# Layer 3's windowed attention in query blocks of ten rows, with another order of work on near tiles

## The chip, the cores and the metric

The kernel runs on one core of a Trainium2 chip. The metric is the device time of one execution in microseconds (us). Before the change it is 3778.4 us, the median of three runs (3774.7 to 3779.35). The engines are TensorE (PE in the profile, its weight loads PEld), VectorE (DVE), ScalarE (ACT), GpSimd (POOL) and SyncE (SP), which issues the DMAs.

## The reference, cut to what matters

Four layers run one after another on `x` of shape (4, 256, 48, 48), each of the form `x = x + layer(group_norm(x))`. Layers 0 to 2 are convolutions, and the change doesn't touch them. Layer 3 is a linear attention with eight heads of 32 channels and three square windows:

```python
q = sigmoid(einsum('bchw,oc->bohw', x, Wq)).reshape(b*h, d, H, W)
k = sigmoid(einsum('bchw,oc->bohw', x, Wk)).reshape(b*h, d, H, W)
v = normalized over the head's channels (einsum('bchw,oc->bohw', x, Wv))
Ik  = integral(k)                                    # 2D running sums
Ikv = integral(einsum('bfhw,bghw->bfghw', k, v))
for w in (1, 2, 4):
    ws  = H // w                                     # windows of 48, 24 and 12
    wk  = box(Ik, ws);  wkv = box(Ikv, ws)           # sums over the window around each pixel
    attn = einsum('bdhw,bdfhw->bfhw', q, wkv)
    norm = einsum('bdhw,bdhw->bhw', q, wk)
    outs.append(attn / (norm[:, None] + 1e-6))
return einsum('bchw,oc->bohw', concatenate(outs), Wout) + bout
```

A sum over a window of `(q.k) v` is the same as masked scores times values. The kernel computes it in that form: scores of all keys against all queries, times a 0/1 mask for each window, times `v`.

## The kernel before

Keys come in tiles of 128: 8 rows x 16 columns (`a` is the block of rows, `c` the column third). Queries come in blocks of 8 rows, `rb`, with 48 columns. The half-widths of the windows are 24, 12 and 6, so a tile is *near* when the narrowest window (`wi` = 2) sees it, and *far* otherwise. For each tile, TensorE computes scores of four heads as two pairs, each pair in a tile of two PSUM banks; VectorE and ScalarE move them into `sm`, one for each window, under the masks; GpSimd makes the narrowest window's from the widest one's; and two tiles later (`LAG`) TensorE multiplies them with `v` into three accumulators.

```python
RB = 8; NRB = H // RB; NB = RB * W
HALVES = [24, 12, 6]; KC = P // RB; LAG = 2

# pools of layer 3
tc.tile_pool(name="kvp", bufs=2 * NRB, ...)          # keys and values of a block of rows
tc.tile_pool(name="smp", bufs=2 * (LAG + 1), ...)    # masked scores
tc.tile_pool(name="ps_s", bufs=2, space=PSUM, ...)   # scores: one tile of two banks for a pair
tc.tile_pool(name="ps_acc", bufs=1, space=PSUM, ...)

# ... cut ...
def rows_seen(wi, a, rb):
    h = HALVES[wi]
    return (max(0, a * RB - h + 1 - rb * RB), min(RB, a * RB + RB + h - rb * RB))

# Block.scores(pr, a, c): for each pair pr a PSUM tile s
for j in range(2):
    head = slice((2 * pr + j) * D, (2 * pr + j + 1) * D)
    pe.matmul(s[:, j, 0 : (r1 - r0) * (c1 - c0)],
              kvs[self.b, self.ct, a][0][head, c, :],
              self.qs[head, r0:r1, c0:c1], start=True, stop=True)

# Block.masked(a, c, ss)
f0, f1 = max(0, c * KC + KC - HALVES[0]), min(W, c * KC + HALVES[0] + 1)
full = abs(a - rb) * RB + RB <= HALVES[0]     # every row of the block sees all rows of the tile
many = seen(NW - 1, a, rb)                    # near

def middle(s, tiles):      # the second window, on VectorE, straight from the bank
    if full and many:
        of_banks(s, tiles, 1, rows_seen(1, a, rb), cols_seen(1, c))
def copy(s, tiles):        # the widest window where no mask is needed, on ScalarE
    if full:
        act.copy(view(tiles, 0, (r0, r1), (f0, f1)), s[:, :, :, f0 - c0 : f1 - c0])
def widest(s, tiles):      # the rest of the widest window, on VectorE
    if not full:
        of_banks(s, tiles, 0, *all0)
        return
    for p0, p1 in ((c0, f0), (f1, c1)):
        if p0 < p1:
            of_banks(s, tiles, 0, (r0, r1), (p0, p1))

first, second = zip(ss, pairs)
copy(*first)
middle(*second)
copy(*second)
middle(*first)
widest(*first)
widest(*second)
for tiles in pairs:
    # GpSimd: the narrowest window (near) or the second one (far), from the widest
    ...

# the main loop: near and far tiles of a block alternate
ss = [blocks[i].scores(pr, a, c) for pr in range(NPR)]
ahead.append(blocks[i].masked(a, c, ss))
if n >= LAG:
    for wi in (1, 0, 2):
        if wi in sms[0]:
            blocks[i].sums(wi, a, c, sms)      # of the tile two places back
advance()                                      # a step of the jobs beside it
```

The jobs that `advance` moves on are the projections of the next image, the running sums of the keys (`k_sums`), the norms (`norms`) and the output of finished blocks (`finish`). They share the engines with the main loop.

Of the kernel before, what the change touches and what calls it, by code (L numbers as in the profile page):

```python
# [21 lines left out]
P = 128  # L22
B, C, H, W = 4, 256, 48, 48
HW = H * W
# [56 lines left out]
NKT = NRB * NKC  # L81

# [63 lines left out]
def conv_preact_kernel(  # L146
# [76 lines left out]
    o_d = [dram.tile([NRB, P, NW * NB], F32, tag=f"o{b}", name=f"o_d{b}") for b in range(B)]  # L223
    n_d = [dram.tile([NRB, HEADS, NW, NB], F32, tag=f"n{b}", name=f"n_d{b}") for b in range(B)]
    r_d = [dram.tile([NRB, HEADS, NW, NB], F32, tag=f"r{b}", name=f"r_d{b}") for b in range(B)]
# [1257 lines left out]
    with (  # L1483
        tc.tile_pool(name="wts3", bufs=1, reuse_waits="tile") as wts,
        tc.tile_pool(name="kvp", bufs=2 * NRB, reuse_waits="tile") as kvp,
# [21 lines left out]
        zeros = wts.tile([P, NB], BF16, name="zeros")  # L1507
# [63 lines left out]
        def norms(b, rb):  # L1571


            sums = []

            def load(ct):
                chans = slice(ct * P, (ct + 1) * P)
                hi = scr.tile([P, NW, RB, W], F32, tag="nhi", name="nhi")
                lo = scr.tile([P, NW, RB, W], F32, tag="nlo", name="nlo")
                qf = scr.tile([P, RB, W], F32, tag="nq", name="nq")  # L1580
                sync.dma_start(
                    out=qf.rearrange("p r w -> p (r w)"),
                    in_=q_d[b][chans, rb * NB : (rb + 1) * NB],
                )
                for wi, h in enumerate(HALVES):

                    y0 = rb * RB + h - 1
                    n = max(0, min(RB, H - y0))
                    if n > 0:
                        sync.dma_start(  # L1590
                            out=hi[:, wi, 0:n], in_=kb_d[b][wi, chans, y0 : y0 + n, :]
                        )
                    if n < RB:
                        sync.dma_start(
                            out=hi[:, wi, n:RB],
                            in_=kb_d[b][wi, chans, H - 1 : H, :].to_broadcast([P, RB - n, W]),
                        )

                    y0 = rb * RB - h - 1
                    n = min(RB, max(0, -y0))  # L1600
                    if n < RB:
                        sync.dma_start(
                            out=lo[:, wi, n:RB], in_=kb_d[b][wi, chans, y0 + n : y0 + RB, :]
                        )
                return hi, lo, qf

            last = min(rb + HALVES[0] // RB, NRB - 1)
            yield from wait_for(
                *((what, b, ct, at) for what, at in (("kb", last), ("q", rb)) for ct in range(NCT))
            )  # L1610
            loaded = [load(ct) for ct in range(NCT)]
            yield FETCH
            for hi, lo, qf in loaded:
                for wi, h in enumerate(HALVES):
                    n = min(RB, max(0, h + 1 - rb * RB))
                    if n < RB:
                        pool.tensor_sub(hi[:, wi, n:RB], hi[:, wi, n:RB], lo[:, wi, n:RB])
                yield 1
                for wi in range(NW):
                    pool.tensor_mul(hi[:, wi], hi[:, wi], qf)  # L1620
                sums.append(hi)
                yield 1
            yield 1
            yield from bank(1)
            ps = ps_m.tile([P, 512], F32, tag="st", name="norm_ps")
            for ct in range(NCT):
                for wi in range(NW):
                    pe.matmul(
                        ps[D * wi : D * (wi + 1), 0:NB],
                        head_sel[:, ct, :],  # L1630
                        sums[ct][:, wi].rearrange("p r w -> p (r w)"),
                        start=(ct == 0),
                        stop=(ct == NCT - 1),
                    )
            yield 1
            ns = scr.tile([D * NW, NB], F32, tag="ns", name="ns", bufs=1)
            act.copy(ns, ps[0 : D * NW, 0:NB])
            yield 1
            for wi in range(NW):
                sync.dma_start(out=n_d[b][rb, :, wi, :], in_=ns[D * wi : D * wi + HEADS])  # L1640
            nn = HEADS * NW * NB // P
            nr = scr.tile([P, nn], F32, tag="nr", name="nr")
            flat = [d[b][rb].rearrange("h w n -> (h w n)") for d in (n_d, r_d)]
            sync.dma_start(out=nr, in_=flat[0].rearrange("(p n) -> p n", n=nn))
            yield FETCH
            dve.tensor_scalar_add(nr, nr, ATTN_EPS)
            dve.reciprocal(nr, nr)
            yield 1
            sync.dma_start(out=flat[1].rearrange("(p n) -> p n", n=nn), in_=nr)
            made.add(("norm", b, rb))  # L1650
# [12 lines left out]
        def load_q(b, ct, rb):  # L1663
            qs = qp.tile([P, RB, W], F32, tag="qs", name="qs")
            sync.dma_start(
                out=qs.rearrange("p r w -> p (r w)"),
                in_=q_d[b][ct * P : (ct + 1) * P, rb * NB : (rb + 1) * NB],
            )
            return qs

        def rows_seen(wi, a, rb):

            h = HALVES[wi]
            return (
                max(0, a * RB - h + 1 - rb * RB),
                min(RB, a * RB + RB + h - rb * RB),
            )
# [5 lines left out]
        class Block:  # L1683


            def __init__(self, b, ct, rb, qs):
                self.b, self.ct, self.rb, self.qs = b, ct, rb, qs
                self.tiles = tiles_of(rb)
                self.todo = [
                    [(a, c) for a, c in self.tiles if seen(wi, a, rb)] for wi in range(NW)  # L1690
                ]
                self.accs = self.stage = None

# [18 lines left out]
            def masked(self, a, c, ss):  # L1712
# [8 lines left out]
                            [P, 2, RB, min(W, KC + 2 * HALVES[wi])],  # L1721
# [15 lines left out]
                def times_mask(engine, wi, rows, cols, dst, src):  # L1737
                    mr = rb * RB + rows[0] - (a * RB - HALVES[wi] + 1)
# [14 lines left out]
                full = abs(a - rb) * RB + RB <= HALVES[0]  # L1753
# [7 lines left out]
                def copy(s, tiles):  # L1761
                    if full:
                        act.copy(
                            view(tiles, 0, (r0, r1), (f0, f1)), s[:, :, :, f0 - c0 : f1 - c0]
                        )

                def widest(s, tiles):
# [3 lines left out]
                    for p0, p1 in ((c0, f0), (f1, c1)):  # L1771
                        if p0 < p1:
                            of_banks(s, tiles, 0, (r0, r1), (p0, p1))
# [4 lines left out]
                copy(*first)  # L1778
                middle(*second)
                copy(*second)  # L1780
                middle(*first)
                widest(*first)
# [13 lines left out]
            def begin(self):  # L1796
                self.accs = [
                    ps_acc.tile([P, NB], F32, tag=f"acc{i}", name=f"acc{i}") for i in range(NW)
                ]
                self.stage = op.tile([P, NW, NB], F32, tag="stage", name="stage")  # L1800

                for acc in self.accs[1:]:
                    pe.matmul(acc, zeros[:, 0:P], zeros, start=True, stop=False)
# [23 lines left out]
        def tiles_of(rb):  # L1827
# [4 lines left out]
                for a in sorted(range(NRB), key=lambda a: abs(a - rb))  # L1832
# [8 lines left out]
        def prepare(i):  # L1841

            b, ct, rb = order[i]
            yield from wait_for(("norm", b, rb))
            yield from take("o")
            o = op.tile([P, NW, NB], F32, tag="o", name="o", bufs=1)
            sync.dma_start(out=o.rearrange("p w n -> p (w n)"), in_=o_d[b][rb])
            yield from take("res")
            res = scr.tile([P, NCT, RB, W], F32, tag="res", name="res")
            sync.dma_start(  # L1850
                out=res,
                in_=x3_d[b][:, rb * RB : (rb + 1) * RB, :].rearrange("(ct p) r w -> p ct r w", p=P),
            )
            rcs = []
            for t in range(NCT):
                yield from take("rc")
                rc = op.tile([P, NW, NB], F32, tag="rc", name="rc")
                for g in range(HG):
                    sync.dma_start(
                        out=rc[g * D : (g + 1) * D].rearrange("p w n -> p (w n)"),  # L1860
                        in_=r_d[b][rb, t * HG + g]
                        .rearrange("w n -> (w n)")
                        .partition_broadcast(D),
# [4 lines left out]
        def finish(i, stage):  # L1868


            b, ct, rb = order[i]
            yield 1
            if ct == 0:
                sync.dma_start(out=o_d[b][rb], in_=stage.rearrange("p w n -> p (w n)"))
# [11 lines left out]
            for mo in range(NCT):  # L1886
                yield from bank(2)
                ps = ps_m.tile([P, 512], F32, tag="st", name="out_ps")[:, 0:NB]
# [18 lines left out]
                out=out[b, :, rb * RB : (rb + 1) * RB, :].rearrange("(ct p) r w -> p ct r w", p=P),  # L1907
# [4 lines left out]
        order = [(b, ct, rb) for b in range(B) for ct in range(NCT) for rb in range(NRB)]  # L1912
# [11 lines left out]
        seen_first = HALVES[0] // RB + 1  # L1924
# [6 lines left out]
        LOADS = {2: (0,), 3: (1, 2), 4: (3, 4), 5: (5,)}  # L1931
# [20 lines left out]
        def midway(i):  # L1952

            b, ct, rb = order[i]
            if (b, ct) == (0, 0) and 0 < rb <= NRB - seen_first:
                a = seen_first - 1 + rb
                until(("k", 0, 0, a), ("v", 0, a))
                load_kv(0, 0, a)
            if ct == NCT - 1:
                start(prepare(i))  # L1960
            if i + 1 < len(order):
                nb, nct, nrb = order[i + 1]
                until(("q", nb, nct, nrb))
# [88 lines left out]
```

## Time and profile before

| what | before |
|---|---|
| time, median of 3 | 3778.4 us |
| span of the profiled execution | 3775.4 us |
| TensorE / VectorE / ScalarE / GpSimd busy in the span | 86% / 66% / 27% / 40% |
| layer 3: first scores to the last instruction | 1429.5 to 3771.8 us |
| score matmuls in the trace | 5760, busy 832.5 us |
| sums into the accumulators in the trace | 13440, busy 880.5 us |
| VectorE's masks out of the banks | 2592, busy 1135.8 us |
| ScalarE's copies out of the banks | 1152, busy 594.9 us |
| GpSimd's masks | 1152, busy 853.3 us |

Busy time is the union of the records of a group, so matmuls that overlap count once. Each f32 matmul of the program shows as two records in the trace. All instructions carry line 142, that of a helper that records them, so groups are told apart by their tiles: `s` is scores, `sm` masked scores, `acc` the accumulators, `stage` a finished block. In the group lines, the number after the bar is busy time and mean duration in ns, then the idle time of the engine just before and what ended it. A line of the timeline has start, duration, engine, operation and count, and in brackets the idle time before it with its releaser.

### The profile page before, as it was taken

The numbers are of one execution on the slowest core, as the hardware profiler recorded it, in microseconds if no ns is written. First come the engines' busy times: TensorE is split into PE (matmuls) and PEld (weight loads), VectorE is DVE, ScalarE is ACT, GpSimd is POOL, SyncE is SP. The second block draws the span as 40 slices with busy tenths as digits, with TensorE's granted clock in tenths as the row PEclk, the third lists the DMA queues.
The fourth block names the chain that finished last, engine by engine and source line by source line (L and its number), as shares of the span: only waits on it lengthen the run. The fifth ranks groups of instructions, "written<-read, shape, count | busy, mean of one in ns | idle before, by whom it ended". The sixth has DMA issues, their size and how long they took to land. (4 is left out here: it accounts for less than half of the span.)

```text
span 3775.4 us, 68847 instructions
## 1 busy us (share of the span) xinstructions
PE 3264.8 (86%) x26498; PEld 1879.4 (50%) x26498; DVE 2487.2 (66%) x5119; ACT 1036.2 (27%) x2025; POOL 1518.1 (40%) x2184
## 2 busy tenths in 40 slices
PE   3688898998996788988889889899899899989998
PEld 2467686786784564433334334344443344444443
DVE  7876587587583366777666567756577766556665
ACT  0012111111113322433222333332344332233331
POOL 0000120020020034778765486755365766344332
PEclk9798999999997899999999899999999999999999
DMA  7745323324324313345434243533223444101122
GB/s 250 238 135 170 100 104 116 109 95 125 109 75 124 102 70 108 125 136 159 125 103 131 90 136 122 164 97 108 78 95 123 139 116 116 47 31 53 41 60 60
DMA packets 373019, 423.04 MB, mean 112 GB/s; under 512 B 129076, under 2 KB 328532, under 8 KB 371540
## 3 DMA queue, kind: packets, MB, share of 16 engines
q1 hardware_dynamic: 371491, 416.32, 35.6%
q8 instruction: 211, 3.46, 0.4%
q0 software_dynamic: 144, 1.52, 0.2%
q14 instruction: 117, 0.95, 0.1%
q10 hardware_dynamic: 1056, 0.79, 0.1%
HBM read 288.79 MB, written 131.25 MB: 111 GB/s over the span
## 5 line engine op out<-in xcount | busy, mean ns | idle before, releaser
L142 DVE TENSOR_TENSOR sm<-s,masks 128x112 f32<-128x112 f32 (+10 forms) x2592 | 1135.8, 493 | 765.5 <-PE s L142 321.1
L142 POOL TENSOR_TENSOR sm<-sm,masks 128x432 f32<-128x432 f32 (+14 forms) x1152 | 853.3, 755 | 936.5 <-ACT sm L142 672.0
L142 PE MATMUL s<-qs,ks 32*128 32x320 f32 (+3 forms) x5760 | 832.5, 500 | 200.1 <-DVE sm L142 151.2
L142 ACT COPY sm<-s 128x528 f32<-128x528 f32 (+2 forms) x1152 | 594.9, 535 | 1470.7 <-PE s L142 1169.9
L142 PE MATMUL acc<-sm,vs 128*32 128x384 f32 (+18 forms) x13440 | 880.5, 385 | 16.1 <-POOL sm L142 15.8
L142 PEld LDWEIGHTS s<-qs,ks 32*128 32x128 f32 x5760 | 374.1, 185 | 604.7 <-DVE sm L142 232.8
L142 PE MATMUL cv<-vx,wt 128*128 128x288 f32 x2080 | 559.3, 425 | 90.7 <-DVE vx L142 49.1
L142 PEld LDWEIGHTS acc<-sm,vs 128*32 128x32 f32 x13440 | 355.2, 110 | 551.3 <-issue 348.6
L142 PEld LDWEIGHTS cv<-vx,wt 128*128 128x128 f32 x2080 | 402.4, 198 | 212.4 <-issue 53.6
L142 POOL MEMSET v<- 128x16 f32 (+1 forms) x120 | 18.6, 215 | 725.7 <-DVE vx L142 635.7
L142 PE MATMUL cv<-v,wl 128*128 128x384 f32 x1152 | 224.5, 354 | 24.4 <-DVE x L142 9.2
L142 PEld LDWEIGHTS cv<-v,wl 128*128 128x128 f32 x1152 | 214.8, 195 | 34.6 <-issue 16.1
L142 POOL TENSOR_TENSOR pt<-pt 128x144 f32<-128x144 f32 x336 | 187.4, 558 | 22.8 <-DVE pt L142 0.5
L142 POOL TENSOR_TENSOR v<-l2v,v 128x384 fp32r<-128x384 f32 x96 | 109.2, 1168 | 130.2 <-ACT v L142 121.4
L142 POOL TENSOR_TENSOR nhi<-nhi,nq 128x384 f32<-128x384 f32 x144 | 148.3, 1058 | 0.0
L142 PE MATMUL cv<-pad,wl 128*128 128x384 bf16 x864 | 143.1, 327 | 0.0
L142 PE MATMUL out_ps<-o,wout_sb 128*128 128x384 f32 x288 | 122.8, 509 | 9.4 <-DVE o L142 5.4
L142 PE MATMUL out_ps<-stage,wout_sb 128*128 128x384 f32 x288 | 117.3, 489 | 0.4 <-DVE stage L142 0.4
L142 PE MATMUL proj_ps<-wv_sb,xn 128*128 128x256 f32 x288 | 89.5, 438 | 32.3 <-ACT vt L142 19.1
L142 DVE TENSOR_TENSOR vx<-v 128x868 f32<-128x868 f32 x112 | 115.4, 1056 | 0.5
L142 PE MATMUL ap<-seen,xT 120*128 120x120 f32 (+3 forms) x832 | 113.5, 293 | 0.0
L142 PEld LDWEIGHTS <-wl 128*128 128x128 bf16 x864 | 83.8, 97 | 59.1 <-issue 0.4
(162 smaller groups left out, 2859.0 us busy)
## 6 DMA issues: line engine op xcount, KB each, us to landing
wt<-wt SPq DMA_DIRECT2D x48, 768.0 KB
kb_d<-pt SPq DMA_DIRECT2D x48, 576.0 KB
rc<-r_d SPq DMA_DIRECT2D x192, 144.0 KB
nhi<-kb_d SPq DMA_DIRECT2D x120, 192.0 KB
nlo<-kb_d SPq DMA_DIRECT2D x88, 192.0 KB
o_d<-stage SPq DMA_DIRECT2D x24, 576.0 KB
o<-o_d SPq DMA_DIRECT2D x24, 576.0 KB
wl<-wl_d SPq DMA_DIRECT2D x16, 768.0 KB
```

The source lines that it names most:

```text
L142: return lambda *args, **kwargs: self.tc.keep_in_program_order(op(*args, **kwargs))
```

## The change

There are two parts. First, the query blocks of the main loop become ten rows high (`QR`, so five blocks, the last one of eight rows); keys, projections and norms stay in blocks of eight. ScalarE's copy is decided row by row: the rows `g0` to `g1` that see the whole key tile are copied if they are more than a third, and VectorE masks the other rows. Second, on near tiles VectorE begins with the first pair and ScalarE with the second, and then they change banks. Both are for fewer and larger instructions and for shorter times in which one engine waits for another's bank.

What goes with it: keys and values get nine buffers instead of twelve, and their loads for the next half are issued a block earlier; the norms load the second operand one half at a time into one buffer; the reciprocals go to memory in an order that a block of ten rows can be read from, in eight stores instead of one.

```diff
+QR = 10
+QROWS = [(y, min(H, y + QR)) for y in range(0, H, QR)]
+NQB = len(QROWS)
+QN = QR * W
...
-        tc.tile_pool(name="kvp", bufs=2 * NRB, reuse_waits="tile") as kvp,
+        tc.tile_pool(name="kvp", bufs=NRB + 3, reuse_waits="tile") as kvp,
...
         # norms
+                lo = scr.tile([P, NW, RB, W], F32, tag="nlo", name="nlo", bufs=1)
...
+            lo = load_less(0)
             yield FETCH
-            for hi, lo, qf in loaded:
+            for ct, (hi, qf) in enumerate(loaded):
+                if ct > 0:
+                    yield FETCH
...
+                if ct + 1 < NCT:
+                    lo = load_less(ct + 1)
...
-            sync.dma_start(out=flat[1].rearrange("(p n) -> p n", n=nn), in_=nr)
+            for h in range(HEADS):
+                sync.dma_start(
+                    out=r_d[b][h, :, rb * NB : (rb + 1) * NB].rearrange("w (s n) -> w s n", n=nn),
+                    in_=nr[h * NW * 4 : (h + 1) * NW * 4],
+                )
...
         def rows_seen(wi, a, rb):
             h = HALVES[wi]
-            return (
-                max(0, a * RB - h + 1 - rb * RB),
-                min(RB, a * RB + RB + h - rb * RB),
-            )
+            y0, y1 = QROWS[rb]
+            return max(0, a * RB - h + 1 - y0), min(y1, a * RB + RB + h) - y0
...
-                full = abs(a - rb) * RB + RB <= HALVES[0]
+                g0 = max(r0, a * RB + RB - HALVES[0] - self.y0)
+                g1 = min(r1, a * RB + HALVES[0] + 1 - self.y0)
+                full = 3 * (g1 - g0) > r1 - r0
...
                 def copy(s, tiles):
                     if full:
                         act.copy(
-                            view(tiles, 0, (r0, r1), (f0, f1)), s[:, :, :, f0 - c0 : f1 - c0]
+                            view(tiles, 0, (g0, g1), (f0, f1)),
+                            s[:, :, g0 - r0 : g1 - r0, f0 - c0 : f1 - c0],
                         )
...
                     for p0, p1 in ((c0, f0), (f1, c1)):
                         if p0 < p1:
-                            of_banks(s, tiles, 0, (r0, r1), (p0, p1))
+                            of_banks(s, tiles, 0, (g0, g1), (p0, p1))
+                    for p0, p1 in ((r0, g0), (g1, r1)):
+                        if p0 < p1:
+                            of_banks(s, tiles, 0, (p0, p1), (c0, c1))
...
                 first, second = zip(ss, pairs)
-                copy(*first)
-                middle(*second)
-                copy(*second)
-                middle(*first)
-                widest(*first)
+                if full and many:
+                    middle(*first)
+                    widest(*first)
+                    copy(*second)
+                    copy(*first)
+                    middle(*second)
+                else:
+                    copy(*first)
+                    copy(*second)
+                    widest(*first)
                 widest(*second)
...
-        LOADS = {2: (0,), 3: (1, 2), 4: (3, 4), 5: (5,)}
+        LOADS = {1: (0,), 2: (1, 2), 3: (3, 4), 4: (5,)}
```

## The prediction

> **What bounds the kernel now.** I read the page's totals first, then the stage that the change touches, then the groups by shape, the waits and a few microseconds of the timeline.
>
> ```profile
> span 3775.4 us, 68847 instructions
> PE 3264.8 (86%) x26498; PEld 1879.4 (50%) x26498; DVE 2487.2 (66%) x5119; ACT 1036.2 (27%) x2025; POOL 1518.1 (40%) x2184
> ```
>
> The scores of layer 3 start at 1429.5 us. A table of one stretch, from there to the last instruction, gives the stage (columns: length, then busy time and instructions of each engine, granted clock, DMA share, GB/s):
>
> ```profile
> 1429.50:3771.80 2342.30, 2081.84 (x20664) 943.38 (x20664) 1547.90 (x3296) 773.85 (x1537) 1364.18 (x1886) 0.97 0.34 103
> ```
>
> So 2342 of 3775 us are at stake; the other layers are untouched. TensorE looks 89% busy (2081.84/2342.30) and VectorE 66%. The waits in that stretch say that this 89% isn't all work (who waited on whom, total us, times, longest):
>
> ```profile
> DVE sm L142 <- PE s L142: 321.1, 342, 9.2
> DVE sm L142 <- ACT sm L142: 266.9, 181, 5.5
> PEld s L142 <- DVE sm L142: 232.8, 348, 4.5
> PEld s L142 <- ACT sm L142: 167.2, 190, 2.3
> PE s L142 <- DVE sm L142: 151.2, 243, 3.9
> ```
>
> VectorE waits for scores while TensorE's next scores wait for VectorE: a ring, in which neither is full. The timeline shows one turn, a near tile (24 sums) and a far tile (8 sums):
>
> ```profile
> 3601.31 1.41 PE L142 MATMUL s<-qs,ks 32*128 32x320 f32 x8
> 3602.22 0.51 ACT L142 COPY sm<-s 128x400 f32<-128x400 f32 x1 [3.41 <-PE s L142]
> 3602.65 1.61 PE L142 MATMUL acc<-sm,vs 128*32 128x312 f32 x24
> 3602.76 1.78 DVE L142 TENSOR_TENSOR sm<-s,masks 128x448 f32<-128x448 f32 x4 [0.91 <-PE s L142]
> ...
> 3604.38 0.96 PE L142 MATMUL s<-qs,ks 32*128 32x280 f32 x8
> 3605.21 1.39 DVE L142 TENSOR_TENSOR sm<-s,masks 128x560 f32<-128x560 f32 x2 [0.67 <-POOL sm L142]
> 3605.27 0.77 PE L142 MATMUL acc<-sm,vs 128*32 128x336 f32 x8
> 3606.01 1.46 PE L142 MATMUL s<-qs,ks 32*128 32x320 f32 x8
> ```
>
> Eight score matmuls of 320 columns take 0.82 us when nothing holds them (the shortest in the stage); here they take 1.41, because the second pair's bank was still with VectorE. VectorE in turn begins the near tile with the **second** pair, so it stands idle 0.91 us until the last of the eight is done. One turn takes 3606.01 - 3601.31 = 4.70 us, TensorE's own work in it 0.82 + 1.61 + 0.75 + 0.77 = 3.95 us: 0.75 us are lost.
>
> Over the whole stage I took each tile's score group from the timeline, its length less the shortest of its width (0.82 us for 320 columns, 0.93 for 384, 0.75 for 280, 0.85 for 336): 252 us of waiting inside the groups, and 193 us of idle TensorE just before them. **445 us** is the sum that this change can attack.
>
> [...]
>
> ```profile
> L142 DVE TENSOR_TENSOR sm<-s,masks 128x624 f32<-128x624 f32 x256 | 194.9, 802 | 98.3 <-PE s L142 94.2 <-ACT sm L142 3.2 <-POOL sm L142 0.8
> L142 DVE TENSOR_TENSOR sm<-s,masks 128x112 f32<-128x112 f32 x384 | 101.7, 265 | 0.0
> L142 ACT COPY sm<-s 128x528 f32<-128x528 f32 x384 | 229.1, 615 | 489.0 <-PE s L142 382.4 <-DVE sm L142 79.6 <-POOL sm L142 21.6
> L142 ACT COPY sm<-s 128x384 f32<-128x384 f32 x384 | 177.6, 480 | 516.3 <-PE s L142 419.1 <-DVE sm L142 83.4 <-POOL sm L142 9.3
> L142 POOL TENSOR_TENSOR sm<-sm,masks 128x432 f32<-128x432 f32 x96 | 99.5, 1044 | 150.3 <-ACT sm L142 149.6
> L142 POOL TENSOR_TENSOR sm<-sm,masks 128x210 f32<-128x210 f32 x80 | 47.1, 595 | 87.8 <-ACT sm L142 87.6
> ```
>
> From these, per instruction of n elements a partition: VectorE (802 - 265)/512 = 1.05 ns each on top of 148 ns; ScalarE 0.94 on 120; GpSimd 2.02 on 170. In the same way TensorE: scores 0.27 us + 1.72 ns a column (0.82 at 320, 0.93 at 384), sums 0.22 us + 1.63 ns a column (far tiles: 0.68 at 280, 0.85 at 384).
>
> **The change part by part.** Walking the loops for both block heights gives the counts.
>
> *Fewer, taller tiles.* 30 (key block, query block) combinations x 3 columns x 8 become 27 x 3 x 8: 720 tiles become 648. Score and sum columns stay as they are. TensorE loses only fixed parts: 72 x 0.27 = 19 us of scores, 72 x 0.22 = 16 of sums, 16 zero matmuls at 0.25 = 4 us. **-39 us**, on the engine that is nearest to its limit, so I count it whole.
>
> *VectorE.* 2592 mask instructions become 2496, and 851,968 elements become 895,936, since far tiles that were copied whole are now copied only in the rows that see all of the key tile. +43,968 x 1.05 ns = +46; -96 x 0.148 = -14: **+32 us** of work, not of time: VectorE had 794 us idle.
>
> *ScalarE and GpSimd.* Copies 1152 to 1008, about -25 us. GpSimd's masks 1152 to 912 and 36,096 elements fewer: -41 - 73 = -114 us. Both have slack.
>
> *The order on near tiles.* VectorE begins with the first pair, ScalarE with the second, then they change banks. For the turn above at 10 rows: scores of 400 columns 0.27 + 0.69 = 0.96 us, the first bank ready at about 0.5. VectorE does the first pair's middle (560 elements, 0.73) and edge (300, 0.46), some 0.1 less as back-to-back records overlap (four in 1.78 above, 2.04 as a sum): 1.1 us, to 1.6. ScalarE has copied the second pair meanwhile, takes the first (500 elements, 0.59) to 2.3; VectorE does the second to 2.7. TensorE's scores and sums take 0.96 + 1.65 = 2.6. So the first bank is free in time, and the second is wanted 0.48 later, at 3.1: no wait.
>
> *What far tiles leave.* There are 12 kinds of far combinations, 24 tiles each. VectorE's time for both pairs: three copied whole 0.9 us; three of one to three rows 0.5 to 0.8; three for VectorE alone 1.6 to 2.0; three copied in part 1.6 to 1.9, behind a copy of 0.3 to 0.4. TensorE's 0.96 + 0.87 for the large ones covers VectorE alone to within 0.2 us. With part copies the second bank comes free at 0.5 + 0.5 + 1.9 = 2.9, wanted at 1.83 + 0.48 = 2.3: 0.6 lost. I put 0.15, 0.1, 0.2 and 0.6 for the four: a mean of 0.26 against 0.75 now. 0.49 x 288 = **-141 us**.
>
> *Given back.* GpSimd's near masks wait for the first pair's copy, which now ends about 1.8 us later, and a burst of other GpSimd work (three products of 1.06 us for the norms) can sit before them. Some 100 to 190 such bursts at an average of 0.15 us: **+20 us**, an estimate. The norms' second fetch, nine key buffers in place of twelve and the eight small stores of reciprocals: 0, each has several tiles' time to land (DMA share 0.34).
>
> Sum: -39 - 141 + 20 = -160. 3778 - 160 = 3618; I say **3620 us**.
>
> **Rivals.** *The ring only moves.* VectorE grows from 1548 to about 1575 us while the stage shrinks to 2185: 72% full, with projection, scan and output work in its queue between masks. Then each foreign instruction (about 0.7 us) delays a bank, and little of the 141 us is kept: about 3720. For it: 445 us are more than 336 x 0.75 = 252, so a good part comes from elsewhere. Against it: the 0.91 us of idle VectorE are there in every near tile that I looked at. *GpSimd becomes the last wait.* It is 58% busy; two tiles of lag gave the old order some 3.5 us of slack and leave the new one some 2. For it: 57.7 us of sums already wait for GpSimd. Against it: 114 us less work. It would make 3690. *TensorE alone bounds.* If nearly all waiting between near and far goes, the gain nears 250 us: 3530. [...]
>
> **Range and chances.** TensorE's saving is sure to 10 us; the ring's is -50 to -220. That is 3535 to 3705 for 8 in 10. The 2% line is at 3703, so faster by over 2% has 0.81, within 2% 0.15. Slower by 2% needs a wait that I don't see: 0.04.
>
> **What the profile after would show.** Right: score groups of 400 columns with a median near 0.96 to 1.1 us; VectorE's wait for scores well under 321 us; TensorE's idle plus inside waits near 300 us; about 1575 us of VectorE. Wrong: sums waiting for GpSimd by more than 120 us, VectorE's wait for ScalarE grown beyond 267 us (the part copies), ScalarE held at the first pair's copy so long that the stage copies delay the next block's sums, or a clock under 0.95.

## The result and the profile after

The changed kernel takes 3810.88 us, the median of four runs (3799.69 to 3814.2), against 3776.55 us (3771.95 to 3779.35) of the kernel before on the same chip: a ratio of **1.0087, interval [1.0063, 1.0111]**. It is slower by 0.9%. The prediction was 3620 us, 4% faster.

First the totals of the page, and the granted clock in 40 slices of the span (tenths of full speed):

```profile
span 3806.7 us, 63773 instructions
PE 3275.5 (86%) x24082; PEld 1785.0 (47%) x24082; DVE 2550.6 (67%) x4991; ACT 1008.8 (27%) x1857; POOL 1412.6 (37%) x1944
PEclk9799999999997898999898999899989999999999
```

There are 5074 instructions fewer, and the time has grown. Then layer 3 from its first scores to the end of the span, in the columns used before (length, busy time and instructions of PE, PEld, DVE, ACT and POOL, clock, DMA share, GB/s):

```profile
1424.70:3806.70 2382.00, 2099.36 (x18248) 854.92 (x18248) 1611.44 (x3168) 746.60 (x1369) 1258.74 (x1646) 0.94 0.34 101
```

ScalarE (774 to 747) and GpSimd (1364 to 1259) have less to do, as meant. VectorE has more (1548 to 1611), TensorE's busy time hasn't shrunk, and its **clock fell from 0.97 to 0.94**: 276 us of layer 3 ran at a granted clock of 0.50 (half clock below), after 127 us. The waits of the stage, those shown of before and three more; the last line is of the kernel before:

```profile
DVE sm L146 <- PE s L146: 280.9, 244, 7.6
DVE sm L146 <- ACT sm L146: 243.2, 199, 6.6
PEld s L146 <- ACT sm L146: 195.7, 227, 3.7
PEld s L146 <- DVE sm L146: 187.1, 203, 16.3
PE s L146 <- DVE sm L146: 119.3, 119, 15.6
PE s L146 <- ACT sm L146: 92.4, 125, 3.0
DVE o L146 <- DMA rc<-r_d: 47.6, 4, 18.3
PEld acc L146 <- POOL sm L146: 46.3, 72, 3.6
PE s L142 <- ACT sm L142: 13.7, 20, 1.4
```

Line 146 is the helper's line in the changed kernel, 142 in the one before. Of the five waits shown of before, four are smaller in sum; only that of the scores' weight loads for ScalarE grew (167.2 to 195.7). Scores waited for VectorE 243 times (151.2 us) and now wait 119 times (119.3 us), but the longest of these went from 3.9 to 15.6 us: these waits are **fewer and longer**. What scores no longer wait for VectorE they wait for ScalarE, 92.4 us in 125 waits after 13.7 us in 20. In sum scores stood still for these two engines for 165 us before and 212 us after. VectorE's wait for the loaded reciprocals, 5.1 us before, is 47.6 us. A turn in which no other job's work stands on VectorE or TensorE shows the new order at work (start, duration, engine, work; idle time before it):

```profile
3669.06 1.72 PE L146 MATMUL s<-qs,ks 32*128 32x400 f32 x8
3670.05 1.06 DVE L146 TENSOR_TENSOR sm<-s,masks 128x504 f32<-128x504 f32 x2 [0.36 <-PE s L146]
3670.71 0.88 PE L146 MATMUL acc<-sm,vs 128*32 128x400 f32 x8
3670.89 1.08 ACT L146 COPY sm<-s 128x500 f32<-128x500 f32 x2 [1.94 <-PE s L146]
3671.52 1.06 DVE L146 TENSOR_TENSOR sm<-s,masks 128x504 f32<-128x504 f32 x2 [0.41 <-ACT sm L146]
3672.03 1.64 PE L146 MATMUL s<-qs,ks 32*128 32x400 f32 x8 [0.44 <-ACT sm L146]
```

VectorE starts on the first bank at 3670.05, 0.99 us after the group began and not the 0.5 us of the prediction: the first pair's own records run from 3669.06 to 3670.00. VectorE and ScalarE then change banks at 3671.5, and TensorE's next scores wait 0.44 us for ScalarE. Of the groups of 400 columns the shortest takes 0.95 us, the median 1.32.

### The profile page after: what moved, and what is told of

Same layout as the page of the kernel before. It is cut to its first block, busy times and chain, and to the rows that moved or that the text cites. A ratio compares the mean times of both kernels' runs of the same rounds, so it can differ in the third digit from the quotient of the medians.

```text
span 3806.7 us, 63773 instructions
## 1 busy us (share of the span) xinstructions
PE 3275.5 (86%) x24082; PEld 1785.0 (47%) x24082; DVE 2550.6 (67%) x4991; ACT 1008.8 (27%) x1857; POOL 1412.6 (37%) x1944
## 5 line engine op out<-in xcount | busy, mean ns | idle before, releaser
L146 DVE TENSOR_TENSOR sm<-s,masks 128x160 f32<-128x160 f32 (+19 forms) x2496 | 1172.0, 523 | 691.7 <-PE s L146 280.9
L146 POOL TENSOR_TENSOR sm<-sm,masks 128x540 f32<-128x540 f32 (+28 forms) x912 | 760.7, 856 | 1053.8 <-ACT sm L146 554.3
L146 PE MATMUL s<-qs,ks 32*128 32x400 f32 (+11 forms) x5184 | 843.0, 550 | 219.9 <-DVE sm L146 119.3
L146 ACT COPY sm<-s 128x660 f32<-128x660 f32 (+14 forms) x1008 | 565.7, 582 | 1463.5 <-PE s L146 1301.7
L146 PE MATMUL acc<-sm,vs 128*32 128x400 f32 (+25 forms) x11712 | 890.7, 428 | 7.4 <-POOL sm L146 7.4
L146 PEld LDWEIGHTS s<-qs,ks 32*128 32x128 f32 x5184 | 340.7, 190 | 604.5 <-ACT sm L146 195.7
L146 PEld LDWEIGHTS acc<-sm,vs 128*32 128x32 f32 x11712 | 319.0, 113 | 644.4 <-issue 514.3
L146 PE MATMUL out_ps<-o,wout_sb 128*128 128x480 f32 (+1 forms) x240 | 119.2, 579 | 9.2 <-DVE o L146 6.3
L146 DVE TENSOR_TENSOR pt<-cs 128x384 f32<-128x384 f32 x144 | 115.4, 802 | 0.0
L146 PE MATMUL out_ps<-stage,wout_sb 128*128 128x480 f32 (+1 forms) x240 | 114.0, 557 | 0.1
L146 DVE SCALAR_TENSOR_TENSOR x<-cv,alpha,x 128x384 f32<-128x384 f32 x144 | 83.9, 610 | 42.9 <-PE cv L146 42.6
```

Source lines behind the costliest of these rows:

```text
L146: return lambda *args, **kwargs: self.tc.keep_in_program_order(op(*args, **kwargs))
```

## The experiments

Each time below is a median; ratios are to the kernel before, run on the same chip. That kernel's median differed between chips (3774 to 3786 us), so differences between kernels of different batches are taken from ratios, times 3778 us.

**Which half of the change?** First, the changed kernel with blocks of eight rows again, which keeps the new order and all that goes with it:

```diff
-QR = 10
+QR = 8
-        LOADS = {1: (0,), 2: (1, 2), 3: (3, 4), 4: (5,)}
+        LOADS = {2: (0,), 3: (1, 2), 4: (3, 4), 5: (5,)}
```

> Part two alone: blocks of 8 rows, but the new order on near tiles and all that goes with the change (nine key buffers, the norms' second fetch, eight stores). Theory A (the ring between banks did get shorter; what was lost is long waits of TensorE behind VectorE's foreign bursts and behind the reciprocals' DMAs, and the half clock that follows them): 3700 to 3770 us, TensorE waits over 1.9 us in between the 13 (44 us) of before and the 33 (125 us) of after. Rival B (the new order itself costs, since ScalarE's copies of the first pair come late): 3800 us or more, in blocks of 8 too. Rival C (ten rows cost, the order is neutral): 3770 to 3790.

Measured: 3767.68 us, 0.9963 [0.9948, 0.9977]. Then ten rows with the old order:

```diff
-                if full and many:
-                    middle(*first); widest(*first); copy(*second); copy(*first); middle(*second)
-                else:
-                    copy(*first); copy(*second); widest(*first)
+                copy(*first); middle(*second); copy(*second); middle(*first); widest(*first)
                 widest(*second)
```

> Part one alone: blocks of ten rows with the old order on near tiles. Theory A: slower than after, 3840 to 3900 us, as the near tiles lose what the order gave them (0.2 to 0.4 us each of 360). Rival B: faster than after, 3740 or less. Rival C: about as after, 3800 to 3820.

Measured: 3835.52 us, 1.015 [1.0129, 1.0171]. Last, the kernel before with the new order and nothing else (the inverse of this diff):

> The kernel before with the new order on near tiles alone, blocks of 8 rows, and none of what goes with the ten rows (twelve key buffers, no second fetch of the norms, one store). Theory A: near tiles lose 0.4 us each with nothing beside them, of which about a tenth stays, as with all that goes with the change (3768 us): 3735 to 3770 us, a little better than that, as GpSimd waited 29.6 us there for the norms' single buffer and 19.5 for values. Rival B (the order costs): 3790 or more.

Measured: 3748.15 us, **0.994 [0.9925, 0.9954]**. So the order gains some 25 us in either form of the kernel (1.015 to 1.0087 at ten rows, 1 to 0.994 at eight), and the ten rows lose more than that, 56 us on top of the order (0.994 to 1.0087). The order alone is the version that beats both kernels. What else goes with the change costs some 9 us at eight rows by the ratios (0.9963 against 0.994); the two intervals overlap a little, so it may cost nothing.

**The reciprocals and the bursts on VectorE.** The norms of ten-row blocks have a second fetch step for each half, so in an image's first and last blocks the reciprocals are ready only just before they are used. Taking that step out:

```diff
-                if ct > 0:
-                    yield FETCH
```

> The changed kernel without the norms' second fetch pause (four steps), so that a norm takes 16 steps again and not 20, and the reciprocals of the first image are stored and loaded earlier. Theory A: the 47.6 us that VectorE waited for the reciprocals' DMA and most of TensorE's waits of 7 to 16 us go, with some of the half clock: 3740 to 3780 us. If the lateness doesn't matter (rival B or C): 3800 to 3815.

Measured: 3818.63 us, 1.0096 [1.0078, 1.0113]. Most of the wait went and the time stayed. Two lines of its waits, to be set against 47.6 and 46.3 us above:

```profile
DVE o L146 <- DMA rc<-r_d: 13.3, 3, 6.7
PEld acc L146 <- POOL sm L146: 76.9, 96, 6.3
```

34 us of one wait were won, and 31 us more are spent in sums that wait for GpSimd. Of TensorE's waits over 1.9 us, 46 us in sum stand behind another thing, the values' normalization, a run of VectorE instructions with no mask among them. In the timeline after:

```profile
2885.74 0.92 DVE L146 TENSOR_TENSOR vr<-vr,vu 128x24 f32<-128x24 f32 x1
2886.70 1.69 DVE L146 TENSOR_TENSOR vt<-vt,vr 128x768 f32<-128x768 f32 x1
2888.31 0.66 DVE L146 TENSOR_SCALAR xn<-xr,st 128x384 f32<-128x384 f32 x1
2888.89 0.87 DVE L146 TENSOR_TENSOR sm<-s,masks 128x320 f32<-128x320 f32 x2
2889.43 2.36 PE L146 MATMUL s<-qs,ks 32*128 32x480 f32 x8 [4.04 <-DVE sm L146]
```

TensorE idles 4.04 us, and the scores that follow take 2.36 us where 480 columns undisturbed take 1.09. Spreading the normalization over five steps of `advance`, with its last product cut in three:

```diff
             dve.tensor_mul(u, t, r)
+            yield 1
 ...
-            dve.tensor_mul(vt, vt, r...)
+            for kk in range(NKC):
+                dve.tensor_mul(vt[:, kk], vt[:, kk], r...[:, kk])
+                yield 1
```

> The changed kernel with the normalization of the values cut up: its six VectorE instructions, which stand one behind the other in one step, are spread over five steps, the last one in three parts. Theory A: the waits of TensorE behind this burst (46 us in 15 places after, 20 us in 6 before) fall under 15 us and the half clock after them goes: 3760 to 3790 us. Rivals B and C: 3800 to 3820, or slower by the two more instructions a group (18 x 2 x 0.4 us = 14 us of VectorE).

Measured: 3814.39 us, 1.0096 [1.0071, 1.012]. Waits of TensorE over 1.9 us behind this burst fell from 46 to 13 us, and later projections now waited for the store of `vt` instead (three times, 14.1, 10.5 and 15.7 us). A miss, like the one before it: a long wait removed by itself was made up elsewhere.

**The ring by itself.** The next pair leaves out the projections of the following images (image 0's q, k and v stand for all four), the running sums, the norms, the division and the output product; the output is x before layer 3. What remains is scores, masks, sums and the copies of finished blocks.

```diff
-                start(paced(following, 2))                  # projections
+                made.add(...)                               # image 0's are used
-            start(in_turn([k_sums(b, a, mo) ...]))
-        start(in_turn(norms(b, rb) ...))
-                    dve.tensor_mul(src[:, wi], src[:, wi], rcs[t][:, wi])
-                    pe.matmul(ps, wout_sb[...], os[...], ...)
```

> The kernel before without the jobs beside layer 3's main loop: every image uses the queries, keys and values of image 0, and the running sums, the norms, the division and the output product are left out (the output is x before layer 3). What stays is the ring of scores, masks and sums. Theory A (the ring got shorter, and the jobs beside it lost the waits in which they ran unseen): 720 tiles at the lengths they have with nothing beside them (3.2 near to far, 1.8 to 2.1 far to near, 2.9 near to near) make some 1860 us of stage, 3300 us in all. It is the base for the next run.

> The changed kernel with the same left out. Theory A: the undisturbed lengths there (3.0 to 3.2 near, 2.4 and 1.6 far) make 1700 us of stage, so 130 to 170 us less than the bare kernel of before, though the whole kernel is 35 us more: the gain is real and is taken back by the jobs. Rival C (ten rows cost by themselves, as each bank is held longer): within 30 us of the bare kernel of before, or more.

Measured: 3334.34 us, 0.8843 [0.8828, 0.8857], and 3241.22 us, 0.8589 [0.8573, 0.8604]. **Without the jobs the change is a gain of 0.0254, or 96 us.** Later the order alone was put into the bare ring of before:

> The bare kernel of before (no projections of following images, no running sums, norms, division or output product) with the new order on near tiles and its eight rows. Hiding theory (any shorter ring loses its gain to the jobs): 3220 to 3260 us, about what the bare changed kernel has, though with the jobs the order keeps 26 us only. Rows theory (the ten rows are what loses): 3290 to 3320 us, so a gain in the bare ring of the size that the whole kernel shows (15 to 45 us).

Measured: 3210.67 us, 0.8492 [0.8464, 0.852]. The same three stages as rows (before, after, order alone at eight rows):

```profile
1422.10:3330.20 1908.10, 1704.39 (x19297) 776.89 (x19296) 1138.40 (x2600) 650.07 (x1297) 814.03 (x1152) 0.99 0.11 34
```

```profile
1428.40:3242.00 1813.60, 1701.46 (x16976) 693.19 (x16976) 1186.64 (x2504) 616.37 (x1129) 688.56 (x912) 0.97 0.12 35
```

```profile
1420.80:3203.30 1782.50, 1720.65 (x19296) 773.94 (x19296) 1163.96 (x2600) 641.53 (x1297) 796.87 (x1152) 1.00 0.12 36
```

For comparison, the stage of the whole kernel with the order alone (those of before and after stand further up):

```profile
1421.30:3744.70 2323.40, 2115.74 (x20664) 946.43 (x20664) 1591.38 (x3296) 770.10 (x1537) 1374.16 (x1886) 0.97 0.35 104
```

The order takes 133 us off the bare ring (0.8843 to 0.8492) and only 23 us off the whole kernel (0.006). At eight rows nothing else differs. In the kernel before, then, most of the time that the order can remove is needed again once the jobs run. The rows show where: the jobs add about the same busy time to TensorE in all three kernels (377 us before, 395 with the order alone, 398 after). Its idle time between matmuls is 202, 60 and 111 us in the bare rings, and 260, 203 and 278 us with the jobs, so the idle time that the jobs bring is **58, 143 and 168 us**. What the order takes out of the ring, the jobs put back as idle time of TensorE. It fits that the jobs had run unseen in the ring's waits before; on which engine isn't shown.

The ten rows cost 37 us (0.0097) on top of the order even in the bare ring: there TensorE is without matmuls for 111 us instead of 60, and the clock is 0.97 instead of 1.00. Counted from one score group's start to the next, the turns of near tiles take 1103 us with the order alone and 1196 at ten rows, those of far tiles 675 and 612. For each row of queries that a key tile meets, near turns have become cheaper (0.36 to 0.34 us). But keys still come in eights, so that more of the 5680 such rows lie in near tiles (3504 instead of 3072), and 72 of the far tiles meet only one to three rows: their turns take 132 us for 144 rows, 0.92 us a row, where all other far rows take 0.24.

**Which job takes the rest?** Steps between the bare ring and the whole, as pairs: with the projections back; with the output product back too; and with the running sums and norms back, which is the whole without the division.

> The bare kernel of before plus the projections of the following images (each image has its own queries, keys and values again); running sums, norms, division and output product are still left out. All jobs together cost 440 us in the kernel before (3774 - 3334) and 570 in the changed one (3811 - 3241). This and the next three runs ask which jobs the 130 us belong to. Base for the next run: 3430 to 3500 us.

> The bare changed kernel plus the projections. Theory A1 (any job costs more, as there are fewer and fuller steps and less waiting to run in): it gives back about a third of the 130 us, so 40 to 60 us less than its counterpart of before. Theory A2 (the norms and their DMAs are what costs): still 80 to 95 us less. Theory A3 (the projections' bursts on VectorE and the half clock behind them): at most 20 us less.

> The kernel before without running sums, norms and division; projections and output product are in. With its counterpart it parts the output product from the norms: 3540 to 3630 us.

> The changed kernel without running sums, norms and division; projections and output product are in. A1: 0 to 30 us less than its counterpart of before. A2: still 70 to 95 us less, so that the whole loss comes with the norms. A3: about as in the run with projections alone, 0 to 20 us less.

> The kernel before without the division alone: running sums and norms are computed and their reciprocals stored, but nobody loads or multiplies them. Base for the next run: 3700 to 3760 us.

> The changed kernel without the division alone. If the division's loads and products are what costs (VectorE waited 47.6 us for them): 20 to 30 us less than its counterpart of before, as without any norms. If the running sums and norms cost, on VectorE, GpSimd and the DMA queue: 15 to 40 us more than its counterpart.

| what runs | before | after | after less before, us |
|---|---|---|---|
| bare ring | 0.8843 | 0.8589 | -96 |
| + projections | 0.9163 [0.9139, 0.9186] | 0.9069 [0.9046, 0.9092] | -36 |
| + output product | 0.9667 [0.9645, 0.969] | 0.9595 [0.957, 0.962] | -27 |
| + running sums and norms | 0.9965 [0.9952, 0.9978] | 0.9909 [0.9876, 0.9941] | -21 |
| + division: the whole | 1 | 1.0087 [1.0063, 1.0111] | +33 |

All jobs together cost (1 - 0.8843) x 3778 = 437 us before and (1.0087 - 0.8589) x 3778 = 566 us after: **129 us more for the same work**. With the order alone they cost (0.994 - 0.8492) x 3778 = 547 us, so some 110 of the 129 come with the order and some 19 with the ten rows. Along the steps of the table, the projections account for 60 of the 129, the division for 54. The division of before costs 13 us, that of after 67. The steps weren't run with the order alone, so it isn't known how these two shares divide between order and rows.

The division loads reciprocals and multiplies on VectorE. To see whether the products are the cost, all of them (120 at ten rows, 144 at eight) go to GpSimd, in the changed kernel and in the version with the order alone:

```diff
-                    dve.tensor_mul(src[:, wi], src[:, wi], rcs[t][:, wi])
+                    pool.tensor_mul(src[:, wi], src[:, wi], rcs[t][:, wi])
```

> The changed kernel with the division's 120 products on GpSimd in place of VectorE. If the products on VectorE are what costs: 3750 to 3775 us, most of the 66. If the late loads are: GpSimd now waits for them in the same places, its masks come late, 3800 us or more. If GpSimd's own length (about 1.1 us a product, 130 us in all) delays the masks: 3790 to 3820.

> The kernel before with the new order on near tiles and the products on GpSimd, eight rows. Hiding theory: VectorE's 109 us of products, which the shorter ring no longer hides, leave its queue: 3710 to 3740 us against 3748. If they are hidden there: 3740 to 3755. If GpSimd's masks come late: 3755 or more.

Measured: 3807.51 us, 1.0059 [1.0039, 1.008], and 3747.99 us, 0.9907 [0.9888, 0.9926]. Both intervals overlap (the second just) those of the same kernels with the products on VectorE. In the first, the wait for the load moved along:

```profile
POOL o L146 <- DMA rc<-r_d: 45.1, 4, 16.9
```

So the products' place isn't the cost, and neither (by the run without the second fetch) is the load's wait alone. In the second run the hiding theory had asked for 3710 to 3740 us; it missed: taking 109 us of products off VectorE gave no gain that stands clear of the interval. In the traces, TensorE's waits over 1.9 us grow with the division by 50 us at ten rows and by 2 at eight (the table below), five of 6 to 16 us above all. But the run without the second fetch, where this sum was 117 us instead of 134, was not faster. What in the division costs the 54 us isn't settled.

**The clock.** In the traces of before and after, the granted clock is recorded from 54 us on, as 1.00 or 0.50, and it changes only at points of a grid of 3.41 us. A table of slices of this grid around the burst above (columns as for the stage):

```profile
2880.70:2884.11 3.41, 3.17 (x26) 1.31 (x16) 2.02 (x4) 1.81 (x4) 3.17 (x6) 1.00 0.00 0
2884.11:2887.53 3.42, 1.27 (x18) 0.42 (x16) 3.25 (x6) 1.42 (x3) 3.36 (x6) 1.00 0.66 225
2887.53:2890.94 3.41, 1.51 (x8) 0.90 (x8) 3.41 (x6) 0.00 (x0) 3.41 (x4) 0.50 0.65 235
2890.94:2894.35 3.41, 3.41 (x30) 0.99 (x24) 3.09 (x8) 1.46 (x2) 3.41 (x5) 0.50 0.00 0
2894.35:2897.77 3.42, 3.42 (x34) 1.42 (x30) 1.48 (x2) 1.00 (x2) 3.34 (x5) 1.00 0.02 5
```

In the second slice TensorE is busy 1.27 of 3.42 us (0.37), in the third 1.51 (0.44), and after each comes a slice at 0.50. In the same trace the wait of 2.00 us before this group left its slice (from 1508.54 us) busy 1.41 of 3.41 us, 0.41, and the slice behind it, from 1511.95 us, was granted 0.50:

```profile
1511.37 1.79 PE L146 MATMUL s<-qs,ks 32*128 32x400 f32 x8 [2.00 <-DVE sm L146]
```

Over the whole traces of before and after, the median slice ahead of a half-clock stretch was busy 0.35 and 0.36. Of the slices at 1.00 that another at 1.00 followed, the least busy was busy 0.45 before (from 286.1 us) and 0.47 after (from 890.7 us). But 10 of the 46 half-clock stretches of before and 17 of the 70 of after came behind slices busy 0.45 or more, and what brought these isn't known. Counted in layer 3:

| kernel | stage, us | waits of TensorE over 1.9 us: count, us | at half clock, us |
|---|---|---|---|
| before | 2346 | 14, 50 | 127 |
| before without the division | 2342 | 13, 48 | 130 |
| order alone | 2323 | 17, 61 | 146 |
| after, eight rows | 2341 | 20, 64 | 166 |
| after without the division | 2321 | 31, 84 | 229 |
| after | 2382 | 35, 134 | 276 |
| bare ring before / order alone / after | 1908 / 1783 / 1814 | 1, 7 / 1, 6 / 9, 18 | 37 / 16 / 101 |

The ten-row kernels are set apart by long waits and half clock, with the jobs or without. Were TensorE the bound throughout and its work twice as long at half clock, the extra (276 - 127)/2 = 75 us of lost TensorE time would be more than the whole loss; that is an upper estimate (the records of the norms' matmuls, `norm_ps`, took a median of 847 ns at 0.50 and 486 at 1.00 in both traces). To test it, 18 times eight matmuls of zeros that nothing reads were put behind the values' normalization in the changed kernel, to keep the slices there busy:

```diff
+            ps = self.ps_tile()
+            for _ in range(8):
+                pe.matmul(ps[:, 0:480], warm[0][:, 0:P], warm[0][:, 0:480], start=True, stop=True)
```

> The changed kernel with eight matmuls on zeros (0.25 us each, 2 us) put into TensorE's queue where it waits behind the normalization of the values, 18 times; their result is read by nobody. Clock theory (a stretch of 3.4 us in which TensorE is busy for less than about 0.47 is followed by one at half clock, and ten rows make more of them: 44 stretches, 276 us against 22, 127 us): these places lose their half clock, 10 to 15 stretches less, and the run gets 10 to 35 us shorter (3775 to 3800) although TensorE has 36 us more to do. If the half clock has nothing to do with the waits, or costs nothing: the same number of stretches, and 3810 to 3845 us.

Measured: 3803.2 us, 1.0081 [1.0064, 1.0098], no different from 1.0087. Waits behind the burst fell from 46 to 27 us, half clock only from 276 to 259 us. The filling changed the clock too little to price it: what half clock costs here stays an estimate.

**One more order.** On far tiles that are copied, VectorE's rest of the second pair was put before its rest of the first, so that the two engines work on different banks there too:

```diff
+                elif full:
+                    copy(*first)
+                    widest(*second)
+                    copy(*second)
+                    widest(*first)
```

> The kernel before with the new order on near tiles, and the same on far tiles that are copied: ScalarE copies the first pair while VectorE masks the second pair's edge, then they change banks. The second bank comes free some 0.4 us earlier on 192 tiles. If the jobs take most of it, as of the near tiles' gain: 3725 to 3750 us; if it stays: 3680 to 3715; if ScalarE's second copy now waits for VectorE's foreign work: 3750 to 3770.

Measured, on top of the order alone: 3749.59 us, 0.9915 [0.9885, 0.9945], against 0.994 [0.9925, 0.9954] without it. No gain that stands clear of the interval.

## Why the prediction was wrong, point by point

**Given back, +20 us: the step that failed most.** The runs put 129 us there, and of the 193 us between the sum of -160 and the +33 measured, 109 lie here. It counted one kind of disturbance (GpSimd bursts ahead of near masks) and let the other jobs cost what they had cost before. In its place the runs show jobs that bring 168 us of idle time to TensorE instead of 58. But the 445 us that "this change can attack" weren't free time. The nested kernels show it: the order is worth 133 us where nothing else runs and 23 us where the jobs do. (The sum itself was a little high: by the single records it is 222 us inside the groups and 200 before them, 422.) The prediction's own rival, that the ring only moves, named this mechanism at 3720 us, and leaned on a reading that pointed the right way (VectorE fuller, with foreign work in its queue). The argument that set it aside was 0.91 us of idle VectorE in the near tiles looked at; the one shown, at 3601 us, lies in the last image, where no projection runs beside the ring.

**The ring, -39 - 141 = -180 us: right in direction, sized at about twice.** The bare rings give -96, the other 84 of the 193 us. The order alone gave -133 there (at eight rows), close to the -141, but its first step was wrong, so that closeness is partly luck; the ten rows gave +37 instead of -39. Both terms:

- *First bank ready at 0.5.* Measured 0.94 of the group's 0.95 us at 400 columns. The step halved the time of four heads to get that of two. But a pair alone takes nearly as long as both: at 3601.31, in the prediction's own fence, the first pair's records run 0.81 us of 1.41, and ScalarE's copy starts 0.91 us after the group. Everything after that ("to 1.6", "to 2.3", "to 2.7") is late by some 0.45 us or more: in the turn shown ScalarE leaves the first bank at 2.91, and VectorE the second, wanted at 3.1, at 3.52.
- *Ten rows, -39 of fixed parts.* Fewer matmuls did come (24082 records for 26498), yet ten rows added 37 us in the bare ring. The count of 648 tiles was right, but not what they cost: only 24 of the 72 tiles saved are near ones (384 to 360), and the 72 tiles of one to three rows, which got 0.1 us of waiting each, take 0.92 us a row. How much of the 37 us is that and how much the lower clock isn't parted.

**VectorE +32, ScalarE -25, GpSimd -114 us of work: right.** VectorE's masks grew from 1135.8 to 1172.0 us, ScalarE fell by 27 and GpSimd by 105. The estimate of about 1575 us for all of VectorE was short of the 1611 measured: the masks' 36 us came, and the rest of its work grew by 27 us as well.

**The norms' second fetch, nine key buffers and eight stores, "0".** Wrong as a reading of the waits (reciprocals 5.1 to 47.6 us); but removing that wait gained nothing, so it isn't shown as a cause.

**GpSimd as the last wait: no.** Sums waited 57.7 us for it before and 46.3 after. **TensorE alone as the bound: no**; even the bare ring after has 111 us without matmuls.

**The clock: the marker came.** 0.94 in the stage is under the 0.95 named, with TensorE busy 88% of the stage (2099.36/2382.00) after 89%; 53 of the 70 half-clock stretches of the trace stand behind slices busy less than 0.45.

**The markers.** Groups of 400 columns have a median of 1.32 us instead of 0.96 to 1.1, and idle plus inside waits, by the single records, are 470 us after 422 before, instead of 300: both said plainly that the ring hadn't loosened. VectorE's wait for scores fell as asked, 321.1 to 280.9, while the time grew. It was a poor marker: VectorE's work grew by 64 us meanwhile, and TensorE's scores waited longer.

**What stays open:** what in the division costs 54 us more in the changed kernel, which of the jobs' work brings back TensorE's idle time, how much of the loss is the half clock, and where the waits freed without the second fetch and with the spread normalization went in full.

## What to carry to other kernels

Before counting the waits of a ring as gain, ask what else runs beside it: build the ring without its side jobs, before and after, and don't expect its gain in the whole kernel (here 23 of 133 us stayed). The shortest score groups took 0.82 us at 320 columns, 0.95 at 400 and 1.09 at 480, less than in proportion, so larger tiles save fixed parts; but where their height doesn't fit the other side's (ten rows of queries, eight of keys) count the thin tiles that arise, and here the longer waits (134 us over 1.9 us each, after 50) also came with more half clock (276 us after 127). When a change has two parts, run each alone: here the order is worth keeping (0.994) and the ten rows are not.

## What the runs showed of the hardware

- Two heads' scores take nearly as long as four heads': at 400 columns 0.94 us for the first pair's records and 0.95 us for both pairs together. When nothing holds them, their first records start 6 to 7 ns apart (in the group at 1453.85 us of after), so holding the second pair back saves nothing for the first: in the turn at 3669.06 us the first pair took 0.94 us all the same, and the group 1.72.
- Half clock came behind waits shorter than one 3.41 us slice of the clock's grid: in the trace of after, a wait of 2.00 us left its slice busy 0.41, and the next was granted 0.50. Some 1.9 us without matmuls within one slice leave it busy (3.41 - 1.9)/3.41 = 0.44, and the least busy slice at 1.00 with another at 1.00 behind it was busy 0.45 before and 0.47 after; the 4.04 us wait above lies across two slices, busy 0.37 and 0.44, with 0.50 behind both. Half clock also came behind slices busy 0.45 or more, 10 times of 46 before and 17 of 70 after.
